# Weighted sums divided two banks at a time and added by GpSimd, in a two-layer graph attention kernel

## The chip, the cores and the metric

The kernel runs on one core of one Trainium2 chip. The metric is the device time of one execution in microseconds (us), the median of several runs. The kernel before was run three times: 2948.39, 2948.5 and 2950.46 us.

A core has five engines that work side by side, each through its own queue in order: TensorE (PE in the profile; its weight loads are PEld), VectorE (DVE), ScalarE (ACT), GpSimd (POOL) and SyncE (SP), which issues most of the transfers. The queues meet at semaphores: an instruction that waits holds up all that is queued behind it on its engine.

## The reference

The input x has 128 graphs of 64 nodes with 768 features, adj the 128 adjacency matrices of 64 x 64. All is fp32. Two layers follow each other, each with a residual and a layer norm.

```
layer 0:  p = softmax(h h^T / sqrt(768)) * adj;  attn = p / (sum(p) + 1e-10)
          ctx = upper(attn) (h Wl + bl) + diag(attn) (h Ws + bs) + lower(attn) (h Wr + br)
          x  = layernorm(x + relu(layernorm(ctx) * gamma + beta))
layer 1:  q, k, v = x Wq + bq, x Wk + bk, x Wv + bv       (12 heads of 64)
          s = q k^T / sqrt(64) + beta * adj;  s = -9e15 where adj is not > 0
          x  = layernorm(x + softmax(s) v)
```

## The kernel before

**Blocks.** The 8192 tokens are worked on in 16 blocks of 512 (four tiles t of 128 tokens, two graphs in a tile). The large products (self, left, right, values, queries and keys) are done with a seven-product scheme in place of eight: a block's transposed rows and each weight matrix are split in halves both ways, sums of the quarters are formed, and partial results in PSUM are shared. The sums of the rows (`combined`, L316 to L328) are made by GpSimd. For the left and right side the scheme is applied twice from the fourth block on: `both_sides` with `nested` (L419) has 49 sub-products (i, j), and `second_level` (L330) makes the second sums, q, on GpSimd, 13 blocks in all.

**The order of a block.** In the main loop (L1022 on) the stages of neighbouring blocks follow each other on TensorE: turn n of the loop has the two sides of block n+1 (left and right), its self product, the values of block n (with the context of block n+1 in between), and three projections of block n's queries and keys, one for each group of heads hg, four heads in each. A stage calls hooks at places that the loop lists (`at(left, 5, weighted, p, 1)`, with p = n-1): `scores`, `weighted` and `finish_by_act` of block p, transfers. Keys of the two-side stage run from 0 to 27 over its 49 sub-products; the places of `right` begin at 14.

In the two-side stage the matrices come in the order i = 7, 1, 2, 6, 5, 4, 3. The sub-products of one matrix are interleaved with those of the next: (i,6), (i,5), (i,7), then (next,1), (next,2), then (i,4), (i,3). Those with j = 1, 6, 7 are one matmul (two passes in the profile), the others two. Sub-products 1, 6, 7 and 4 of a matrix accumulate in one PSUM bank X, which is evicted after each; so (i,7) must wait until X is evicted after (i,6). Evictions are VectorE additions of 384 columns (L437).

**Queues of small work.** What belongs to other stages is put in three queues of entries, `first`, `urgent` and `lazy`, and `step` (L135), called after each sub-product, emits from them. Here "emits" means that the instruction gets its place in its engine's queue. The rules that matter: one step emits at most one plain entry (a piece of VectorE work), taken from the first queue that has one; entries of the kinds "act", "gap" and "tiny" may go along with it; after sub-products 5, 1 and 4 the step is light and emits no plain entry. "after" entries wait until `first` is empty. A gap entry does nothing but take a step.

**Scores (L814).** q k^T of four heads goes to two PSUM tiles; VectorE multiplies each with m8, the mask that also holds 1/8 (L836), and then, as entries of `urgent`, adds the second mask (L857), takes maxima (L858) and subtracts them (L859). ScalarE makes exponentials (L850), written so that two VectorE transposes (L854) end the turn.

**Weighted sums (L863).** The products of probabilities and values (with a column of ones for the denominators) go to four PSUM tiles of one bank, one for each pair of tiles h and head row r. Four entries of `first`, `added(h, r)`, follow, each a reciprocal of denominators and four operations that scale one head and add it to the rows:

```
nc.vector.reciprocal(rz, ps[:, :, :, HD])
...
nc.vector.scalar_tensor_tensor(res[:, r, c, hg, :], ps[:, t, k, 0:HD], rz[:, t, k : k + 1],
                               res[:, r, c, hg, :], ALU.mult, ALU.add)
```

**The last layer norm (`finish_by_act`, L894).** For the block before, ScalarE sums each of the four tiles ("after" entry, L934), VectorE makes the mean (L909, "tiny"), ScalarE sums squares (L937), VectorE the variance (L912, "tiny"), ScalarE a root, VectorE the factors (L918, L919), ScalarE norms the rows (L923), GpSimd issues the stores (L927). Two gaps stand between the sums and L909 and between the squares and L912. In the two-side stage it is queued at place 16, one place after the last `weighted` (place 15).

**Buffers.** `x1_p` holds the rows of two blocks, eight tiles. `wst` has 19 buffers for streamed weights. [...] `ps_st` four (X and Y, two each), `ps_mm` four one-bank buffers for scores, weighted sums, context, layer 0's products and transposes.

**Prologue.** Before the loop the weights are loaded, their quarters' differences are formed by VectorE (`prepare`, L192) and those for queries and keys are stored for streaming.

## Time and profile before

| | |
|---|---|
| median of three runs | 2948.5 us |
| profiled execution: its time, its span | 2945.44, 2943.7 us |
| TensorE clock granted, mean | 0.995 |
| TensorE matmuls busy | 98% of the span, 17578 instructions |
| VectorE busy | 1990.9 us, 68% |
| ScalarE busy | 1123.3 us, 38% |
| GpSimd busy | 729.8 us, 25% |
| L889, scale and add a head (VectorE) | 768 x 277 ns |
| L836, scores times mask (VectorE, 512 elements from PSUM) | 96 x 684 ns |
| L857, second mask (VectorE, 1024 elements) | 48 x 1221 ns |
| L451, addition on GpSimd, 384 elements | 52 x 1000 ns |
| period of a late block | 179.7 us |

The span is from the first instruction to the last, and 1.7 us of the execution lie around it. Busy times overlap. TensorE's matmuls are pipelined and their ends are modelled, so its 98% is read with care: what counts is the distance from one start to the next. A wait that the lists put down to an engine may belong to another semaphore that the instruction waits for as well; where the two could be mixed up, the timelines of the engines are laid side by side.

### The profile page before, as it was taken

The page shows a single profiled execution, that of the slowest core. Times are in us where ns is not written, and L with a number is a line of the kernel's source. Part 1 is how long each engine was busy: PE and PEld are TensorE (multiplying, and loading weights), DVE is VectorE, ACT ScalarE, POOL GpSimd, SP SyncE. Part 2 cuts the span into 40 slices and gives each one's busy share as a digit, 9 for nine tenths or more (in the row PEclk, how much of TensorE's full clock was granted, in tenths as well). Part 3 has the DMA queues.
Part 4 walks back from the last instruction along what each step waited for, and adds up shares of the span by engine and source line. Part 5 has one row for each costly group of instructions (what it writes and reads, how often), then busy time and mean ns, then how long its engine had stood idle before and what let it go on. Part 6 is the DMA issues. An engine that isn't in the chain of part 4 may idle for free.

```text
span 2943.7 us, 49954 instructions
## 1 busy us (share of the span) xinstructions
PE 2881.4 (98%) x17578; PEld 1935.1 (66%) x17578; DVE 1990.9 (68%) x4034; ACT 1123.3 (38%) x2114; POOL 729.8 (25%) x879
## 2 busy tenths in 40 slices
PE   8999999999999999999999999999999999999997
PEld 5557667575675856658576575766757567585685
DVE  5857777676676766767667576666767667676656
ACT  0004324344243542434434344443434424354254
POOL 3133122305123141321404124051230513313110
PEclk9999999999999999999999999999999999999998
DMA  9778786949669495775957759486694966849442
GB/s 329 222 247 266 230 247 181 266 135 284 160 193 248 138 292 152 207 237 157 277 149 231 216 168 271 138 254 188 183 262 136 287 158 196 247 136 289 139 127 90
DMA packets 440278, 613.18 MB, mean 208 GB/s; under 512 B 53584, under 2 KB 416720, under 8 KB 440032
## 3 DMA queue, kind: packets, MB, share of 16 engines
q1 hardware_dynamic: 362096, 493.57, 55.7%
q10 hardware_dynamic: 60848, 44.05, 8.1%
q0 software_dynamic: 17088, 72.37, 6.7%
q8 instruction: 143, 2.34, 0.3%
q14 instruction: 103, 0.84, 0.1%
HBM read 539.43 MB, written 77.27 MB: 209 GB/s over the span
## 4 chain that ended last, share of the span: by engine, by line
PE 90%; ACT 3%; DVE 3%; POOL 2%; DMA 2%; issue 1%; SPq 0%; DVEq 0%; ACTq 0%
PE ps_X L383 35%; PE ps_Y L383 26%; PE ps_Y L636 11%; PE ps_X L636 10%; PE ps_ctx L675 3%; ACT eT L850 2%; PE sc L832 2%; PE ps_y L879 2%; PE u L526 1%; POOL q L336 1%; ACT L850 1%; ACT uqk L801 1%; POOL q L335 0%; DVE o L889 0%; DMA bs<-in_L_gnn_b_self_dram 0%
## 5 line engine op out<-in xcount | busy, mean ns | idle before, releaser
L383 PE MATMUL ps_X<-xT,wqk 128*128 128x256 f32 x1728 | 395.9, 381 | 9.5 <-ACT uqk L801 9.5
L850 ACT ACTIVATE eT<-s 32x256 f32<-32x256 f32 x768 | 317.8, 414 | 184.7 <-DVE s L859 174.6
L383 PEld LDWEIGHTS ps_X<-xT,wqk 128*128 128x128 f32 x1728 | 325.8, 190 | 67.0 <-ACT uqk L801 16.2
L316 POOL TENSOR_TENSOR S<-hT 128x768 f32<-128x768 f32 x16 | 28.9, 1807 | 1132.9 <-PE ps_Y L383 1102.1
L383 PE MATMUL ps_Y<-S,wqk 128*128 128x256 f32 x1152 | 264.3, 379 | 0.0
L680 ACT ACTIVATE unused<-o 128x768 f32<-128x768 f32 x60 | 50.6, 844 | 499.6 <-DVE o L677 305.2
L383 PEld LDWEIGHTS ps_Y<-S,wqk 128*128 128x128 f32 x1152 | 218.9, 190 | 29.8
L437 DVE TENSOR_TENSOR lr<-ps_Y,u_deep 128x384 f32<-128x384 f32 x273 | 152.0, 557 | 107.5 <-PE ps_Y L636 81.4
L636 PE MATMUL ps_Y<-wlr,q 128*128 128x384 f32 x546 | 208.6, 491 | 0.0
L383 PE MATMUL ps_X<-wv,xT 128*128 128x384 f32 x576 | 195.0, 489 | 0.0
L801 ACT ACTIVATE uqk<-ps_X,bq 128x256 f32<-128x256 f32 x144 | 68.1, 473 | 325.1 <-PE ps_X L383 323.9
L383 PE MATMUL ps_X<-ws,hT 128*128 128x384 f32 x540 | 181.2, 490 | 2.8 <-DVE u L414 2.8
L809 DVE TENSOR_TENSOR q<-ps_Y,uqk 128x256 f32<-128x256 f32 x144 | 61.0, 423 | 178.0 <-ACT uqk L801 89.4
L889 DVE SCALAR_TENSOR_TENSOR o<-ps_y,rz,o 128x64 f32<-128x64 f32 x768 | 165.0, 277 | 6.8
L636 PE MATMUL ps_X<-wlr,q 128*128 128x384 f32 x364 | 151.0, 497 | 14.8 <-issue 6.2
L383 PEld LDWEIGHTS ps_X<-wv,xT 128*128 128x128 f32 x576 | 108.2, 190 | 80.8 <-issue 8.4
L383 PEld LDWEIGHTS ps_X<-ws,hT 128*128 128x128 f32 x540 | 103.2, 191 | 75.5 <-DVE u L414 3.4
L437 DVE TENSOR_TENSOR u_deep<-ps_X,lr 128x384 f32<-128x384 f32 x195 | 107.2, 550 | 67.4 <-PE ps_X L636 65.7
L636 PEld LDWEIGHTS ps_Y<-wlr,q 128*128 128x128 f32 x546 | 101.6, 190 | 67.2
L414 DVE TENSOR_TENSOR u<-ps_X,bv 128x384 f32<-128x384 f32 x96 | 53.4, 556 | 131.2 <-PE ps_X L383 131.2
L383 PE MATMUL ps_X<-S,wqk 128*128 128x256 f32 x576 | 138.2, 385 | 0.0
L383 PE MATMUL ps_Y<-xT,wqk 128*128 128x256 f32 x576 | 135.6, 385 | 0.0
(247 smaller groups left out, 5484.8 us busy)
## 6 DMA issues: line engine op xcount, KB each, us to landing
wlr<-lr_d SPq DMA_DIRECT2D x819, 192.0 KB, 3.4
wqk<-qk_d SPq DMA_DIRECT2D x672, 192.0 KB, 2.4
wv<-d_v SPq DMA_DIRECT2D x192, 192.0 KB, 2.9
ws<-d_s SPq DMA_DIRECT2D x180, 192.0 KB, 5.9
wv<-in_L_gnn_Wv_dram SPq DMA_DIRECT2D x144, 192.0 KB, 4.1
ws<-in_L_gnn_W_self_dram SPq DMA_DIRECT2D x135, 192.0 KB, 5.4
xa<-in_x_dram SPq DMA_DIRECT2D x64, 384.0 KB, 5.3
out_dram<-o POOLq DMA_DIRECT2D x62, 384.0 KB, 6.3
```

The source lines that it names most:

```text
L383: nc.tensor.matmul(ps, lhsT=a, rhs=b, start=(c == 0 and i in (1, 2, 5)), stop=(c == len(fs) - 1), skip_group_check=True)
L414: evicted[nm] = nc.vector.tensor_tensor(u, ps, bias[nm][:, b * HALF : (b + 1) * HALF], ALU.add)
L437: nc.vector.tensor_tensor(dst, view(ps), add, ALU.add)
L636: nc.tensor.matmul(ps, lhsT=a, rhs=b, start=(k == 0 and j in (1, 2, 5)), stop=(k == len(fs) - 1), skip_group_check=True)
L675: nc.tensor.matmul(ps[g * L : (g + 1) * L, 0:HALF], lhsT=blk["aT"][:, t, g * L : (g + 1) * L], rhs=blk["lr"][t][:, g, cols], start=True, s ...
L680: nc.scalar.activation(unused(), o[t], AF.Identity, accum_out=total[:, t : t + 1])
L801: nc.scalar.activation(u, ps, AF.Identity, bias=bias["qk"[j]][:, c : c + 1])
L809: nc.vector.tensor_tensor(dst, ps, part, ALU.add)
L832: nc.tensor.matmul(sc[r][g * L : (g + 1) * L, t, c, :], lhsT=q[rows, c, tok], rhs=k[rows, c, tok], start=True, stop=True)
L850: nc.scalar.activation(e[cols, :, rows], pairs[rows, :, cols], AF.Exp)
L879: nc.tensor.matmul(y[r, h][cols, t, c, :], lhsT=eT[rows, 2 * h + t, c, cols], rhs=v[rows, 2 * h + t, g, hg + c * HC, :], start=True, stop= ...
L889: nc.vector.scalar_tensor_tensor(res[:, r, c, hg, :], ps[:, t, k, 0:HD], rz[:, t, k : k + 1], res[:, r, c, hg, :], ALU.mult, ALU.add)
```

## The change

- `ps_mm` has two buffers of two banks in place of four of one bank; each user takes a pair (`two_banks`).
- `weighted`: one PSUM tile for each head row r, with both pairs of tiles. Two entries, `added(r)`: VectorE takes the reciprocals, multiplies all heads at once into a tile `shares` in SBUF, and GpSimd adds that to the rows.
- `scores`: the weights and the bias of the queries are scaled by 1/8 in the prologue (four ScalarE copies and a small VectorE operation). So VectorE adds one mask to the scores on the way out of PSUM; m8 and L857 fall away.
- Context: both halves of a tile in one pair of banks, one VectorE operation of 768 columns in place of two of 384.
- A block's rows are one tile of `x1_p` in place of four; `wst` has 17 buffers, not 19, which makes room for `shares`.

```diff
-    x1_p = ctx.enter_context(tc.tile_pool(name="x1_p", bufs=2 * T))
+    x1_p = ctx.enter_context(tc.tile_pool(name="x1_p", bufs=2))
...
-    wst = ctx.enter_context(tc.tile_pool(name="wst", bufs=19))
+    wst = ctx.enter_context(tc.tile_pool(name="wst", bufs=17))
...
-    ps_mm = ctx.enter_context(tc.tile_pool(name="ps_mm", bufs=4, space=PSUM))
+    ps_mm = ctx.enter_context(tc.tile_pool(name="ps_mm", bufs=2, space=PSUM))
...
+    nc.vector.tensor_scalar(bias["q"], bias["q"], 1.0 / math.sqrt(HD), None, ALU.mult)
...
+    def two_banks(name):
+
+        return ps_mm.tile([P, 2, 512], F32, tag="mm", name=name)
...
+        if nm == "q":
+
+            for q in b.values():
+                later(key, act(partial(nc.scalar.activation, q[1], q[1], AF.Copy, scale=1.0 / math.sqrt(HD))))
...
-        o = [x1_p.tile([P, D], F32, tag="x1", name=f"o_{n}_{t}") for t in range(T)]
+        blk["x_all"] = x1_p.tile([P, T, D], F32, tag="x1", name=f"o_{n}")
+        o = [blk["x_all"][:, t, :] for t in range(T)]
...
+            ps = two_banks("ps_ctx")[:, :, 0:HALF]
             for h in range(2):
                 cols = slice(h * HALF, (h + 1) * HALF)
-                ps = ps_mm.tile([P, 512], F32, tag="mm", name="ps_ctx")
...
-                nc.vector.scalar_tensor_tensor(o[t][:, cols], o[t][:, cols], dg[:, t : t + 1], ps[:, 0:HALF],
-                                               ALU.mult, ALU.add)
+            halves = o[t].rearrange("p (h c) -> p h c", h=2)
+            nc.vector.scalar_tensor_tensor(halves, halves, dg[:, t : t + 1], ps, ALU.mult, ALU.add)
...
         def one():
-            nc.vector.tensor_scalar(m8, at, 0.0, 1.0 / math.sqrt(HD), ALU.is_gt, ALU.mult)
             nc.vector.tensor_scalar(off, at, 0.0, MASKED, ALU.is_le, ALU.mult)
+            nc.vector.tensor_scalar(add, at, 0.0, abeta_c, ALU.max, ALU.mult)
...
-            nc.vector.tensor_tensor(s[:, :, :, r, :], sc[r], m8[:, :, None, :].to_broadcast([P, T, 2, L]), ALU.mult)
+            nc.vector.tensor_tensor(s[:, :, :, r, :], sc[:, r], add, ALU.add)
...
-              lambda: nc.vector.tensor_tensor(s4, s4, add[:, :, None, :].to_broadcast([P, T, 4, L]), ALU.add),
               lambda: nc.vector.tensor_reduce(mx, s8, AX.X, ALU.max),
...
-        y = {(r, h): ps_mm.tile([P, 2, 2, HD + 1], F32, tag="mm", name=f"ps_y{r}") for h in halves for r in range(2)}
+        y = [two_banks(f"ps_y{r}")[:, 0 : len(halves), 0 : 4 * (HD + 1)]
+             .rearrange("p h (t c d) -> p h t c d", t=2, c=2) for r in range(2)]
...
+        def added(r):
+            k = len(halves)
+            rz = st.tile([P, 2, 4], F32, tag="rz1", name="rz1")[:, 0:k, :]
+            shares = yt_p.tile([P, 2, 4, HD], F32, tag="shares", name="shares")[:, 0:k]
+            by_head = y[r].rearrange("p h t c d -> p h (t c) d")
+            nc.vector.reciprocal(rz, by_head[:, :, :, HD])
+            nc.vector.tensor_tensor(shares, by_head[:, :, :, 0:HD], rz[:, :, :, None].to_broadcast([P, k, 4, HD]),
+                                    ALU.mult)
+            res = blk["x_all"][:, 2 * halves[0] : 2 * halves[0] + 2 * k, :]
+            res = res.rearrange("p t (c k r d) -> p t r c k d", c=2, k=HC, r=2)[:, :, r, :, hg, :]
+            nc.gpsimd.tensor_tensor(res, res, shares.rearrange("p h (t c) d -> p (h t) c d", c=2), ALU.add)
+
+        later(("y", n, hg), *[partial(added, r) for r in range(2)], queue=first)
...
+    yt_p = ctx.enter_context(tc.tile_pool(name="yt", bufs=2))
```

More of the change, by code (lines that the diff above doesn't have):

```diff
@@ L280, in transposed @@
     def transposed(src, xT, t):
+        both = two_banks("ps_x").rearrange("p b (c i) -> p b c i", c=4)
         for c0 in range(0, KC, 3):
-            ps = ps_mm.tile([P, 4, P], F32, tag="mm", name="ps_x")
+            ps = both[:, c0 // 3]
             for c in range(3):
@@ L519, in attention0 @@
         freed()
-        u = ps_mm.tile([P, T, L], F32, tag="mm", name=f"u_{n}")
+        u = two_banks(f"u_{n}")[:, 0, 0 : T * L].rearrange("p (t l) -> p t l", t=T)
         for t in range(T):
@@ L574, in sides @@
         freed()
-        aps = ps_mm.tile([P, T, P], F32, tag="mm", name="ps_a")
+        aps = two_banks("ps_a")[:, 0, :].rearrange("p (t m) -> p t m", t=T)
         for t in range(T):
@@ L670, in part @@
             freed()
+            ps = two_banks("ps_ctx")[:, :, 0:HALF]
             for h in range(2):
                 cols = slice(h * HALF, (h + 1) * HALF)
-                ps = ps_mm.tile([P, 512], F32, tag="mm", name="ps_ctx")
                 for g in range(2):
-                    nc.tensor.matmul(ps[g * L : (g + 1) * L, 0:HALF], lhsT=blk["aT"][:, t, g * L : (g + 1) * L],
+                    nc.tensor.matmul(ps[g * L : (g + 1) * L, h, :], lhsT=blk["aT"][:, t, g * L : (g + 1) * L],
                                      rhs=blk["lr"][t][:, g, cols], start=True, stop=True)
-                nc.vector.scalar_tensor_tensor(o[t][:, cols], o[t][:, cols], dg[:, t : t + 1], ps[:, 0:HALF],
-                                               ALU.mult, ALU.add)
+            halves = o[t].rearrange("p (h c) -> p h c", h=2)
+            nc.vector.scalar_tensor_tensor(halves, halves, dg[:, t : t + 1], ps, ALU.mult, ALU.add)
             if by_act:
@@ L742, in mask @@
         at = blk["at"]
-        m8 = l0.tile([P, T, L], F32, tag="m8", name=f"m8_{n}")
-        add = l0.tile([P, T, L], F32, tag="add", name=f"add_{n}")
+        blk["add"] = add = l0.tile([P, T, L], F32, tag="add", name=f"add_{n}")
         off = l0.tile([P, T, L], F32, tag="a", name="off")
-        blk["m8"], blk["add"] = m8, add
         def one():
-            nc.vector.tensor_scalar(m8, at, 0.0, 1.0 / math.sqrt(HD), ALU.is_gt, ALU.mult)
             nc.vector.tensor_scalar(off, at, 0.0, MASKED, ALU.is_le, ALU.mult)
+            nc.vector.tensor_scalar(add, at, 0.0, abeta_c, ALU.max, ALU.mult)
         def two():
-            nc.vector.tensor_scalar(add, at, 0.0, abeta_c, ALU.max, ALU.mult)
             nc.vector.tensor_add(add, add, off)
@@ L824, in scores @@
         s = l1s_p.tile([P, T * 4 * L], F32, tag="s", name="s").rearrange("p (t c r m) -> p t c r m", t=T, c=2, r=2)
-        sc = [ps_mm.tile([P, T, 2, L], F32, tag="mm", name=f"sc{r}") for r in range(2)]
+        sc = two_banks("sc").rearrange("p r (t c m) -> p r t c m", t=T, c=2)
         for t in range(T):
@@ L831, in scores @@
                         tok = slice(t * P + g * L, t * P + (g + 1) * L)
-                        nc.tensor.matmul(sc[r][g * L : (g + 1) * L, t, c, :], lhsT=q[rows, c, tok],
+                        nc.tensor.matmul(sc[g * L : (g + 1) * L, r, t, c, :], lhsT=q[rows, c, tok],
                                          rhs=k[rows, c, tok], start=True, stop=True)
-        m8, add = blk["m8"], blk["add"]
+        add = blk["add"][:, :, None, :].to_broadcast([P, T, 2, L])
         for r in range(2):
-            nc.vector.tensor_tensor(s[:, :, :, r, :], sc[r], m8[:, :, None, :].to_broadcast([P, T, 2, L]), ALU.mult)
-        s4 = s.rearrange("p t c r m -> p t (c r) m")
+            nc.vector.tensor_tensor(s[:, :, :, r, :], sc[:, r], add, ALU.add)
         s8 = s.rearrange("p t c r m -> p (t c r) m")
@@ L861, in scores, with weighted @@
               *([partial(turn, 0), partial(turn, 1)] if pool is None else [lambda: (turn(0), turn(1))]), queue=urgent)
-    def weighted(n, hg, halves=range(2), heads=range(2)):
+    def weighted(n, hg, halves=(0, 1)):
         blk = blocks[n]
@@ L869, in weighted @@
         freed()
-        xt, eT = blk["x"], blk["eT", hg]
-        y = {(r, h): ps_mm.tile([P, 2, 2, HD + 1], F32, tag="mm", name=f"ps_y{r}") for h in halves for r in range(2)}
-        for h in halves:
+        eT = blk["eT", hg]
+        y = [two_banks(f"ps_y{r}")[:, 0 : len(halves), 0 : 4 * (HD + 1)]
+             .rearrange("p h (t c d) -> p h t c d", t=2, c=2) for r in range(2)]
+        for k, h in enumerate(halves):
             for t in range(2):
-                for c in heads:
+                for c in range(2):
                     for r in range(2):
@@ L878, in weighted @@
                             cols = slice(g * L, (g + 1) * L)
-                            nc.tensor.matmul(y[r, h][cols, t, c, :], lhsT=eT[rows, 2 * h + t, c, cols],
+                            nc.tensor.matmul(y[r][cols, k, t, c, :], lhsT=eT[rows, 2 * h + t, c, cols],
                                              rhs=v[rows, 2 * h + t, g, hg + c * HC, :], start=True, stop=True)
-        def added(h, r):
-            ps = y[r, h][:, :, heads[0] : heads[-1] + 1, :]
-            rz = st.tile([P, 2, 2], F32, tag="rz1", name="rz1")[:, :, 0 : len(heads)]
-            nc.vector.reciprocal(rz, ps[:, :, :, HD])
-            for t in range(2):
-                res = xt[2 * h + t].rearrange("p (c k r d) -> p r c k d", c=2, k=HC, r=2)
-                for k, c in enumerate(heads):
-                    nc.vector.scalar_tensor_tensor(res[:, r, c, hg, :], ps[:, t, k, 0:HD], rz[:, t, k : k + 1],
-                                                   res[:, r, c, hg, :], ALU.mult, ALU.add)
-        later(("y", n, hg), *[partial(added, h, r) for h in halves for r in range(2)], queue=first)
+        def added(r):
[10 more added lines that the diff above has]
+        later(("y", n, hg), *[partial(added, r) for r in range(2)], queue=first)
     def finish_by_act(n, tiles=range(T), queue=urgent):
```

## The prediction

> **What bounds the kernel now.** I read the page's busy times first, then the list of waits for TensorE alone, then the timeline of one late block, engine by engine.

> ```profile
> span 2943.7 us, 49954 instructions
> PE 2881.4 (98%) x17578; PEld 1935.1 (66%) x17578; DVE 1990.9 (68%) x4034; ACT 1123.3 (38%) x2114; POOL 729.8 (25%) x879
> ```

> ```profile
> PE ps_X L383 <- ACT uqk L801: 9.5, 16, 0.6
> PE ps_X L383 <- DVE u L414: 8.2, 4, 2.8
> ```

> TensorE sets the time, its matmul count does not change, and VectorE is not the bound on average. So 200 us less VectorE work buys only the small waits of TensorE. In a late block (period 179.7 us) I find them by spacing. A matmul of 384 columns is issued each 0.32 us; what is longer is a wait. Timeline at sub-products (5,6), (5,5), (5,7) of the stage of the two sides, TensorE, then VectorE (start, length in us):

> ```profile
> 1784.88 0.81 PE L636 MATMUL ps_X<-wlr,q 128*128 128x384 f32 x2
> 1785.53 0.81 PE L636 MATMUL ps_Y<-wlr,q 128*128 128x384 f32 x2
> 1786.17 0.81 PE L636 MATMUL ps_Y<-wlr,S 128*128 128x384 f32 x2
> 1787.19 0.88 PE L636 MATMUL ps_X<-wlr,q 128*128 128x384 f32 x2 [0.21 <-issue]
> ...
> 1785.76 0.86 DVE L889 SCALAR_TENSOR_TENSOR o<-ps_y,rz,o 128x64 f32<-128x64 f32 x4
> 1786.54 0.55 DVE L437 TENSOR_TENSOR u_deep<-ps_X,lr 128x384 f32<-128x384 f32 x1
> ```

> The last matmul should come at 1786.82 and comes at 1787.19: 0.37 late, because it accumulates on a bank whose eviction (1786.54) stood behind the additions of the weighted sum. The same reading, at each eviction that follows a sub-product (i,3), gives four such waits a block: behind additions 0.37 twice (before 1762.99 and 1787.19), behind the L859 subtraction 0.62 (before 1770.78), behind a transpose 0.40 (before 1778.4). One wait of 0.76 in the third projection is for ScalarE, busy with exponentials. The rest of a block's waits the change does not touch.

> The chain that ends the previous block's layer norm shares these queues:

> ```profile
> 1788.49 0.84 ACT L934 ACTIVATE unused<-o 128x768 f32<-128x768 f32 x1 [11.42 <-DVE o L889]
> 1792.14 0.19 ACT L934 ACTIVATION_READ_ACCUMULATOR unused<-o 128x1 f32 x1
> 1793.09 0.94 ACT L937 ACTIVATE unused<-o,f 128x768 f32<-128x768 f32 x1 [0.76 <-DVE f L909]
> 1797.12 0.18 ACT L937 ACTIVATION_READ_ACCUMULATOR unused<-o,f 128x1 f32 x1
> ...
> 1791.33 0.56 DVE L437 TENSOR_TENSOR lr<-ps_X,lr 128x384 f32<-128x384 f32 x1
> 1792.36 0.69 DVE L909 TENSOR_SCALAR f<-f 128x4 f32<-128x4 f32 x1 [0.47 <-ACT unused L934]
> 1795.87 0.56 DVE L437 TENSOR_TENSOR lr<-ps_Y,u_deep 128x384 f32<-128x384 f32 x1
> 1797.33 0.21 DVE L912 TENSOR_SCALAR f<-f 128x4 f32<-128x4 f32 x1 [0.91 <-ACT unused L937]
> ```

> The small VectorE steps L909 and L912 are queued just late enough: each waits under 1 us for ScalarE's four sums (3.84 us) and four squares (4.2 us).

> [...] the trace gives 1000 ns for 384 elements (L451) and 1807 for 768 (L316), 2.1 ns per element[...] in the two stretches that hold 2.8 us waits (columns: stretch, length, busy times, granted clock):

> ```profile
> 130.00:142.00 12.00, 9.23 (x24) 5.01 (x23) 10.93 (x21) 0.00 (x0) 0.00 (x0) 0.86 1.09 297
> 162.00:176.00 14.00, 11.21 (x26) 6.01 (x26) 9.60 (x12) 0.00 (x0) 13.34 (x18) 0.76 1.05 386
> 36.00:40.00 4.00, 1.99 (x6) 0.88 (x6) 3.93 (x9) 0.00 (x0) 2.27 (x5) 1.00 1.01 370
> ```

> The last one, with 2.0 us idle, keeps its clock.

> **The change part by part.**
> *Weighted sums.* Per block and head group VectorE loses 4 reciprocals (172 ns) and 16 operations (277 ns) and gets 2 reciprocals and 2 products of 512 elements (684, from L836): 5.12 to 1.71 us. GpSimd gets 2 additions of 512; from L451 and L316 1.27 us each, 122 us in all. An entry of the queue `first` falls from 0.98 us of VectorE (rz to the next operation in the timeline) to 0.81 (0.21, and 0.60, half of the 1.29 us pair of L836 less overlap), and there are two entries, not four.
> *Mask.* L857 (1221 ns, 48) and L749 go; one entry of the chain of scores goes with it.
> *Context.* Two operations of 614 become one of about 1016 (L704 has that size): 13 us of VectorE in all, hidden under TensorE's value products.
> These three free 200 us of VectorE; only the named waits are on the path. Played through the queues' rules, the steps now emit L857 after (7,7), L858 (1,2), additions (7,3) (1,6) (1,7) (2,2), L859 (1,3), exponentials (2,6) (2,5), transposes (2,3) (6,6), additions (5,2) (6,3) (5,6) (5,7), and the timeline has them there. Changed: L858 (7,7), L859 (1,2), additions (7,3) (1,6), exponentials (7,3) (1,6), transposes (1,3) (2,6), additions (5,2) (6,3). What stands before the four evictions, after (7,3), (1,3), (2,3) and (6,3), becomes additions, transpose, nothing, additions. So 0.37+0.62+0.40+0.37 becomes 0.20+0.14+0+0.20 (each shorter by what is shorter in front): 1.2 us gained. In the third projection the exponentials start one step (1.3 us) earlier, but three groups of 1.7 stand before the eviction in place of two: 0.76 becomes about 0.3. Gain per block 1.67; bounds 0.8 and 2.1.

> *What is late next.* Two entries fewer pull the layer-norm chain forward by three sub-products: the sums are queued after (6,3), not (5,7); L909 after (5,7), not (5,4); L912 after (5,3), not (4,7). ScalarE cannot follow. Count from (5,6) at 0. VectorE's second product ends at 1.55, GpSimd's addition, behind L452 (0.33) and the first one, at 2.95; ScalarE is free of its own DMA issues at 3.2 to 3.6 (1788.4 in the trace). Sums end 3.87 later: L909 starts at 6.85 to 7.5 (call it T). It stands in VectorE's queue since 4.05, ahead of the evictions of (4,1), (4,2), (5,4), (5,3). L909 0.2 to 0.6, squares 4.24, so L912 ends at about T+4.7 to T+5.1; only then comes the eviction of (4,6) with 0.65, which (4,7) needs. (4,7) starts at 12.2 to 13.2, against 9.23 undisturbed (sub-products of one matmul, 0.645 us, or two from 2.13 on). Loss 3.0 to 4.0 us in a block; I take 3.5. The gaps are about 0.8 before (4,6) and 2.6 before (4,7).
> Net 3.5 - 1.67 = 1.83 us, in the 13 blocks with this stage: +24. The first two blocks and the last have the projection's gain alone: -2.

> *GpSimd's queue.* The two late additions (2.5 us) stand before the second-level sums of matrices 4 and 3, where GpSimd idles some 1 us between 1781.9 and 1799.1; the last sums come 1.5 to 1.9 us late against a slack of about 1.4: 0 to 0.6 a block. The 3.5 us above cover it; without that cover it is 8 us in all. The early two have idle time (3.69 us before 1768.47).
> *Pairs of banks, two buffers.* Each pair is evicted several us before its slot comes round (scores at 1752.9, next use 1758.2): 0; in the tail, where weighted sums follow each other, -1 to +1.
> *One tile for a block's rows.* The first write (1811.66) now waits for all four stores, issued up to 1803.5 with a median of 6.3 to landing: 0, and VectorE has two steps of slack behind it.
> *17 weight buffers.* Some 0.9 us per tile (63 in 57 us), so 1.8 us less lead; landing takes 3.4 (median), and the waits list shows TensorE waiting for none of these loads: 0, bound +1 a block.
> *Query weights scaled.* Four ScalarE copies of 1152 elements in the prologue, ScalarE idle there but VectorE's differences wait for them: 0 to 3, I take 1. *Tail*: the last addition through GpSimd, +0.8.
> *Clock.* A gap of 2.6 lies between 2.0 (no drop) and 2.8 (drop). A drop costs 1.7 (0.14 x 12) to 3.4 us (0.24 x 14). I expect it in few blocks: +2.

> Sum: 24-2+1+1+2 = +26 on the profiled 2945.4 (span and 1.7 around it), which lies 3.1 below the median of 2948.5: forecast 2974.5, 0.9% slower. A measurement here tells about 0.2% from no change.

> **Rivals.**
> (1) Faster: the layer-norm chain does not block, only the gains show: -1.67 x 13 - 2 = -24, 2925. For it: all the waits of VectorE above are real. Against: ScalarE's 3.87 us of sums cannot fit in the 2.8 us between their new place and L909's. It decides if L909 stays queued behind (5,3); the loss is nought where T is below 3.4 to 3.9.
> (2) GpSimd becomes the bound of the stage: 31 us busy of 57 there, 36 after; with the gains kept and 0.6 lost a block, 2933[...].
> (3) The clock drops in every block: 13 x 2.5 more, 3005. For it: the gap is close to 2.8.
> (4) The shallower weight ring starves TensorE at the stage's end, where transfers crowd: 1 us a block more, 2987.

> **How the numbers follow.** Forecast with few drops 0.60 (its own range 2962 to 2990: losses 3.0 to 4.0, gains 0.8 to 2.1); (3) 0.11; (4) or another added loss 0.07; (1) 0.12; (2) 0.10, split evenly between faster and no change. Slower 0.78, same 0.05, faster 0.17. The range 2930 to 3004 leaves out most of (1) and the worst of (3).

> **What would show it.** Right: in the timeline L909 waits 2 to 3 us on L934 and L912 about as long on L937, with a TensorE gap of some 2.6 us before each (4,7); L885 in pairs; VectorE near 1790 us busy, GpSimd near 850. Wrong: L909 behind (5,3), TensorE's period at 178, or waits for `wlr`, `q` or ScalarE's `uqk` in its list.

## The result and the profile after

The changed kernel takes 3020.5 us, the median of four runs (3018.1 to 3022.4), beside 2949.0 of the kernel before on the same chip: a ratio of 1.0241, with a 95% interval from 1.0224 to 1.0259. The forecast was 2974.5 with a range up to 3004. The sign was right and the size was not: +72 us where +26 was forecast.

The page of the changed kernel, the span and the busy times:

```profile
span 3017.7 us, 49120 instructions
PE 2907.4 (96%) x17578; PEld 1941.9 (64%) x17578; DVE 1830.7 (61%) x3151; ACT 1129.4 (37%) x2120; POOL 828.0 (27%) x981
```

VectorE has lost 160 us of work, GpSimd has gained 98, and TensorE, with the same number of matmuls, has a span 74.0 us longer. Its list of waits (total, times, longest) shows what the time went to:

```profile
PE ps_X L647 <- DVE u_deep L447: 36.0, 26, 2.6
PE ps_X L647 <- POOL lr L461: 11.6, 13, 0.9
PE ps_X L393 <- DVE u L424: 10.5, 5, 3.5
PE ps_X L393 <- ACT uqk L810: 9.1, 31, 1.5
...
PE ps_y L887 <- DVE shares L896: 5.8, 3, 4.5
PE ps_y L887 <- DVE rz L895: 4.5, 4, 2.4
```

The first two stand in the stage of the two sides (L647 is L636 of the kernel before, L447 is L437) and come in each of its 13 blocks, the first twice, once for 2.6 us and once for 0.2. The last two stand in the tail. I measured the stages from the first product of one to the first product of the next in TensorE's record:

| part of the run | before | after | difference |
|---|---|---|---|
| up to the first nested two-side stage | 490.5 | 496.6 | +6.1 |
| the 13 two-side stages, sum | 735.1 | 788.7 | +53.6 |
| a late two-side stage | 56.5 | 60.9 | +4.4 |
| projections of a block | 62.5 | 62.4 | -0.1 |
| projections of the last block | 124.0 | 128.4 | +4.4 |
| tail, from the last values on | 54.7 | 65.4 | +10.7 |
| period of a late block | 179.7 | 184.05 | +4.3 |

In the timeline of one late block, VectorE and then TensorE, the forecast steps are all there (L919 is the mean, L922 the variance; the last number in brackets is the idle time before the instruction):

```profile
1637.61 0.56 DVE L447 TENSOR_TENSOR lr<-ps_Y,u_deep 128x384 f32<-128x384 f32 x1
1640.78 1.04 DVE L919 TENSOR_SCALAR f<-f 128x4 f32<-128x4 f32 x1 [2.62 <-ACT unused L944]
1641.74 0.54 DVE L447 TENSOR_TENSOR u_deep<-ps_X,lr 128x384 f32<-128x384 f32 x1
...
1646.10 0.50 DVE L922 TENSOR_SCALAR f<-f 128x4 f32<-128x4 f32 x1 [2.23 <-ACT unused L947]
1646.51 0.54 DVE L447 TENSOR_TENSOR u_deep<-ps_X,lr 128x384 f32<-128x384 f32 x1
...
1642.38 0.88 PE L647 MATMUL ps_X<-wlr,q 128*128 128x384 f32 x2 [0.89 <-POOL lr L461]
1643.10 0.81 PE L647 MATMUL ps_Y<-wlr,q 128*128 128x384 f32 x2
1643.75 0.81 PE L647 MATMUL ps_Y<-wlr,hT 128*128 128x384 f32 x2
1647.11 1.34 PE L647 MATMUL ps_X<-wlr,q 128*128 128x384 f32 x2 [2.56 <-DVE u_deep L447]
1648.25 1.49 PE L647 MATMUL ps_X<-wlr,S 128*128 128x384 f32 x2
```

VectorE holds L919 for 2.62 us while ScalarE sums, and the eviction at 1641.74 stands behind it; TensorE starts (4,6) 1.05 us late. The list names GpSimd's L461 for that wait, but that ended at 1641.80 and the eviction at 1642.28, just ahead of the matmul at 1642.38. L922 then holds the next eviction, and (4,7) comes 2.72 us late.

What the forecast did not count in every block is in the spacing of the two last rows: two matmuls of 384 columns each, 1.14 us apart where 0.64 is usual. Here are the 3.41 us that hold most of the wait, and the 3.41 us after them (columns: stretch, length, busy times of PE, PEld, DVE, ACT and POOL, granted clock, DMA share, GB/s; the last section says why this length):

```profile
1644.06:1647.47 3.41, 0.85 (x3) 0.30 (x2) 0.96 (x2) 3.35 (x6) 3.33 (x4) 1.00 0.90 288
1647.47:1650.88 3.41, 3.41 (x7) 1.76 (x6) 2.08 (x5) 0.72 (x2) 3.01 (x6) 0.50 0.88 323
```

After the wait the granted clock is 0.50, and TensorE has 7 matmuls in the stretch. Waits of the same length in two of the 13 blocks let the clock stand; after one of them it has 12:

```profile
1278.81:1282.22 3.41, 1.50 (x5) 0.98 (x6) 1.45 (x3) 2.34 (x4) 3.25 (x5) 1.00 0.99 332
1282.22:1285.64 3.42, 3.42 (x12) 1.98 (x11) 2.46 (x7) 2.44 (x3) 2.71 (x6) 1.00 1.00 362
```

Those two stages take 59.2 us, the others 60.9 (one 61.3). The fall costs 1.7 us.

### The profile page after: what moved, and what is told of

Its sections match the earlier page's. It is cut to its first block, busy times and chain, and to the rows that moved or that the text cites. A ratio compares the mean times of both kernels' runs of the same rounds, so it can differ in the third digit from the quotient of the medians.

```text
span 3017.7 us, 49120 instructions
## 1 busy us (share of the span) xinstructions
PE 2907.4 (96%) x17578; PEld 1941.9 (64%) x17578; DVE 1830.7 (61%) x3151; ACT 1129.4 (37%) x2120; POOL 828.0 (27%) x981
## 3 DMA queue, kind: packets, MB, share of 16 engines
q1 hardware_dynamic: 362096, 493.57, 54.7%
## 4 chain that ended last, share of the span: by engine, by line
PE 77%; ACT 11%; DVE 5%; DMA 5%; issue 1%; POOL 0%; SPq 0%; ACTq 0%; DVEq 0%
PE ps_X L393 30%; PE ps_Y L393 23%; PE ps_Y L647 9%; PE ps_X L647 8%; ACT eT L858 5%; PE ps_ctx L686 3%; ACT unused L947 2%; PE sc L841 2%; DMA wlr<-lr_d 2%; ACT unused L944 2%; PE u L536 1%; ACT uqk L810 1%; PE ps_y L887 1%; DMA sq<-x1d 1%; ACT L858 1%
## 5 line engine op out<-in xcount | busy, mean ns | idle before, releaser
L900 POOL TENSOR_TENSOR o<-o,shares 128x512 f32<-128x512 f32 (+1 forms) x102 | 126.4, 1248 | 1388.6 <-DVE shares L896 1309.7
L858 ACT ACTIVATE eT<-s 32x256 f32<-32x256 f32 x768 | 317.8, 414 | 48.3 <-DVE s L866 37.6
L691 ACT ACTIVATE unused<-o 128x768 f32<-128x768 f32 x60 | 50.6, 843 | 507.0 <-DVE o L689 264.9
L447 DVE TENSOR_TENSOR lr<-ps_Y,u_deep 128x384 f32<-128x384 f32 x273 | 152.1, 557 | 140.1 <-PE ps_Y L647 116.9
L647 PE MATMUL ps_Y<-wlr,q 128*128 128x384 f32 x546 | 208.6, 491 | 0.0
L647 PE MATMUL ps_X<-wlr,q 128*128 128x384 f32 x364 | 153.9, 505 | 48.7 <-DVE u_deep L447 33.2
L944 ACT ACTIVATE unused<-o 128x768 f32<-128x768 f32 x62 | 52.3, 843 | 288.2 <-POOL o L900 164.6
L447 DVE TENSOR_TENSOR u_deep<-ps_X,lr 128x384 f32<-128x384 f32 x195 | 107.3, 550 | 82.6 <-PE ps_X L647 80.3
L647 PEld LDWEIGHTS ps_Y<-wlr,q 128*128 128x128 f32 x546 | 100.5, 190 | 68.3 <-DVE lr L447 4.5
L647 PEld LDWEIGHTS ps_X<-wlr,q 128*128 128x128 f32 x364 | 64.0, 190 | 115.8 <-DVE u_deep L447 41.2
```

The costliest lines, as they stand in the source:

```text
L447: nc.vector.tensor_tensor(dst, view(ps), add, ALU.add)
L647: nc.tensor.matmul(ps, lhsT=a, rhs=b, start=(k == 0 and j in (1, 2, 5)), stop=(k == len(fs) - 1), skip_group_check=True)
L691: nc.scalar.activation(unused(), o[t], AF.Identity, accum_out=total[:, t : t + 1])
L858: nc.scalar.activation(e[cols, :, rows], pairs[rows, :, cols], AF.Exp)
L900: nc.gpsimd.tensor_tensor(res, res, shares.rearrange("p h (t c) d -> p (h t) c d", c=2), ALU.add)
L944: later(key, (partial(sums, lambda t, o: nc.scalar.activation(o, xt[t], AF.Identity, accum_out=total[:, t : t + 1])), "after"), GAP, GAP, ...
```

## The experiments

**1. The chain put back to its place.** Three more gap entries between the sums and the mean.

```diff
-              GAP, GAP, tiny(mean),
+              *[GAP] * 5, tiny(mean),
```

> The changed kernel with three more gap entries between the sums and the mean in finish_by_act, which puts the mean (L919) and the variance (L922) back to the places of the kernel before, after (5,4) and (4,7). Theory (the early chain makes the two waits and the half clock behind the second): in the changed kernel they cost 1.05 + 2.72 + 1.77 = 5.5 us in a late block, so 13 blocks give back 68 to 72 us: 2946 to 2956, and a late block's period is 178.5 to 179 us. Rival A (GpSimd, with the additions now on it, is late with the second-level sums, and bounds the stage as soon as VectorE's waits are gone): at most 2 us a block come back, 2994 or more, with waits for GpSimd in TensorE's list. Rival B (17 weight buffers): no change, 3015 to 3025.

Measured: 2965.2 us, ratio 1.0057 (1.0042 to 1.0072). The period of a late block is 178.99, the two-side stage takes 55.85, so the 13 stages cost 726 us where the changed kernel has 789 and the kernel before 735. Of the two waits nothing is left. The mechanism holds, and rivals A and B fall: with the chain late enough, the additions on GpSimd and the ring of 17 leave a block shorter than before. The timeline shows also what A was right about, TensorE, then GpSimd:

```profile
1803.67 0.91 PE L647 MATMUL ps_X<-wlr,q 128*128 128x384 f32 x2 [0.32 <-POOL q L346]
...
1788.97 2.67 POOL L900 TENSOR_TENSOR o<-o,shares 128x512 f32<-128x512 f32 x2
...
1802.63 0.46 POOL L345 TENSOR_TENSOR q<-S 128x128 f32<-128x128 f32 x1
1803.17 0.45 POOL L346 TENSOR_TENSOR q<-q,S 128x128 f32<-128x128 f32 x1
```

The two additions of 2.67 us make the second-level sums of a later matrix late, and TensorE waits 0.49 us for L346, once a block. In the changed kernel the longer waits covered it.

The total missed its expectation by 9 us, for two reasons outside the 13 stages. In turn 1 of the loop the self product of block 2 (the expectation of run 7 calls it block 1) takes 33.3 us, not 27.1, and VectorE shows why:

```profile
387.21 1.02 DVE L601 TENSOR_TENSOR o<-ps_Y,u 128x384 f32<-128x384 f32 x2 [8.22 <-DMA out_dram<-o]
```

The rows of a block are one tile now, and the first write to them waits for all four stores of block 0. The gap entries delay those stores, and block 0's chain has no nested stage to run in. The other is the tail, 68.7 for 65.4, where the same entries stand in the last chains.

**2. The variance alone, one place later.**

```diff
-              GAP, GAP, tiny(variance), act(root), ...
+              *[GAP] * 3, tiny(variance), act(root), ...
```

> The changed kernel with one more gap entry between the squares and the variance, nothing else. The variance is then queued after (4,6), behind that sub-product's eviction. It waits for ScalarE as before, but what stands behind it is needed three sub-products later. Theory with the clock as a cost of its own: the wait before (4,7) goes, and the half clock that follows it too: 13 x (2.72 + 1.77) = 58, so 2962 (2955 to 2970); the wait of 1.05 before (4,6) stays. If the clock's fall has another cause than that wait: 13 x 2.72 = 35, 2985. If the wait only moves to the next eviction: 3010 or more.

Measured: 2962.8 us, ratio 1.0051 (1.0036 to 1.0066). The two-side stage takes 56.6 us, 4.3 less than 60.9: the wait of 2.72 and the 1.7 of half clock went together (the granted clock of the profiled run is 0.993, that of the changed kernel's 0.988). VectorE, then TensorE:

```profile
1798.60 0.55 DVE L447 TENSOR_TENSOR u_deep<-ps_X,lr 128x384 f32<-128x384 f32 x1
1800.91 0.51 DVE L922 TENSOR_SCALAR f<-f 128x4 f32<-128x4 f32 x1 [1.76 <-ACT unused L947]
...
1798.56 0.81 PE L647 MATMUL ps_Y<-wlr,hT 128*128 128x384 f32 x2
1799.20 0.91 PE L647 MATMUL ps_X<-wlr,q 128*128 128x384 f32 x2
```

VectorE still waits 1.76 us at L922. But the eviction that (4,7) needs stands ahead of it, and (4,7) starts at 1799.20, on time. The wait of 1.05 before (4,6), which the edit does not touch, is still there.

**3. The mean one place later,** and with it all that follows.

```diff
-              GAP, GAP, tiny(mean),
+              *[GAP] * 3, tiny(mean),
```

> The changed kernel with one more gap entry between the sums and the mean, which moves the mean behind the eviction of (4,1) and the variance behind that of (4,6). Theory (a wait costs what the next needed eviction behind it loses, not what the waiting instruction waits): both instructions still wait 2 to 3 us on VectorE, but both waits of TensorE go, so it is within 8 us of the kernel with three more entries, 2946 to 2964. If instead the length of VectorE's wait counts, about a third of the gain of three entries comes: 2995 to 3000.

Measured: 2973.4 us, ratio 1.0080 (1.0063 to 1.0097), between the two expectations and nearer the first. The stage takes 56.9 us for most blocks. VectorE waits as long as ever, 2.15 us at L919 and 2.42 at L922 in the block read, and the waits before (4,6) and (4,7) are gone; but a new one of 1.01 stands three sub-products on, before (4,4), whose bank waits for an eviction behind L922, and one of 0.35 before (4,5). So an entry moved by one place takes most of the loss, but a piece of it moves to the next eviction. The right side of block 2 takes 33.9 us for 31.1 besides. Against 2, a later mean makes the squares, and so the variance, later. In the 13 stages that is some 3 of the 11 us between the two runs; that right side makes 6 of them (28.0 in 2), and the last of the 13 stages takes 59.1, with one wait of 1.8 us for weights.

**4. The chain pulled forward in the kernel before,** which leaves out two of the last weighted sum's four entries, so that the chain comes earlier by two.

```diff
-        later(("y", n, hg), *[partial(added, h, r) for h in halves for r in range(2)], queue=first)
+        later(("y", n, hg), *[partial(added, h, r)
+              for h in (halves if hg != 2 or not DEEP - 2 <= n < NBLK - 2 else (0,)) for r in range(2)], queue=first)
```

> The kernel before with two of the four entries of the last weighted sum (hg 2) left out in the 13 blocks with the two-side stage nested: half of that head group's sums are not added to the rows. VectorE has 2 us less work in a block; nothing else of the change is made. The chain's sums, mean and variance are then queued after (6,3), (5,7) and (5,3), as in the changed kernel. Theory: the waits come with the places alone. The sums begin up to 1 us earlier than in the changed kernel, since no addition goes through GpSimd, so a block loses 2 to 5.5 us: 2975 to 3020. Rivals A and B: 2940 to 2950, no loss without the additions on GpSimd and the shallower ring.

Measured: 2996.9 us, ratio 1.0166 (1.0151 to 1.0182): with less work than the kernel before it takes 48 us more. The stages take 58.3 to 61.5 us, 783 in all. TensorE in a late block:

```profile
1820.29 0.81 PE L636 MATMUL ps_Y<-wlr,hT 128*128 128x384 f32 x2
1823.65 1.59 PE L636 MATMUL ps_X<-wlr,q 128*128 128x384 f32 x2 [2.56 <-DVE u_deep L437]
1825.03 1.49 PE L636 MATMUL ps_X<-wlr,S 128*128 128x384 f32 x2
```

The same wait of 2.72 before (4,7), and the spacing of half clock behind it (the last two rows start 1.38 us apart where 0.64 is usual; the granted clock of the run is 0.990, 0.995 in the kernel before), without a pair of banks, an addition on GpSimd or a shallower ring. So the number of entries ahead of the chain is enough to make the loss of the blocks.

**5. Pairs of banks alone, in the kernel before.** Each user of `ps_mm` takes a pair; the context keeps its operation for each half.

```diff
+            both = two_banks("ps_ctx")
             for h in range(2):
-                ps = ps_mm.tile([P, 512], F32, tag="mm", name="ps_ctx")
+                ps = both[:, h]
                 ... two products, then one scalar_tensor_tensor on ps
```

> The kernel before with ps_mm as two buffers of two banks, each user taking a pair, and nothing else of the change (four entries of a weighted sum, two masks, additions by VectorE). The prediction's value: 0, tail -1 to +1, so 2948 to 2950. Against it, from the trace of the changed kernel: transposes that wait for two evictions of a pair (prologue +2.4, last block +4.4) and weighted sums of one half in the tail, which follow each other and take a pair for each head row (+3 to +6): 2957 to 2963, with the blocks' period at 179.7 as before.

Measured: 3019.3 us, ratio 1.0240 (1.0226 to 1.0254). That is as slow as the whole change, and for another reason, as the stages show: the two sides take 56.5 as before, the values 37.5 where both kernels have 33.6. The first entry of TensorE's list of waits, and the place in the timeline:

```profile
PE ps_ctx L681 <- DVE o L683: 46.5, 61, 1.8
```

```profile
1871.89 0.87 PE L681 MATMUL ps_ctx<-lr,aT 128*64 128x384 f32 x4
1873.50 0.87 PE L681 MATMUL ps_ctx<-lr,aT 128*64 128x384 f32 x4 [0.74 <-DVE o L683]
```

The products of the second half wait until VectorE has read the first half in the other bank of the pair. The change avoids this by its one operation for a tile. So this run did not measure the pairs as the change uses them, and the agreement of its total with the changed kernel's is chance.

**6. 17 weight buffers alone, in the kernel before.**

```diff
-    wst = ctx.enter_context(tc.tile_pool(name="wst", bufs=19))
+    wst = ctx.enter_context(tc.tile_pool(name="wst", bufs=17))
```

> The kernel before with 17 buffers for streamed weights in place of 19, nothing else. Theory: no wait for weights, 2946 to 2952 and a period of 179.7. Rival (the shallower ring starves TensorE at the stage's end): 1 us a block, 2962.

Measured: 2946.2 us, ratio 0.9993 (0.9984 to 1.0001). A late period is 179.8. The 13 stages take 737.2 us for 735.1, with two waits for weights of 0.6 us at most: the ring costs next to nothing and is not the cause.

**7. The tail's additions on VectorE,** with the chain put back in the 13 blocks only (and one gap entry more before the variance of block 0).

```diff
+        deep = queue is urgent and len(tiles) == T and n + 2 >= DEEP
-              GAP, GAP, tiny(mean),
+              *[GAP] * (5 if deep else 2), tiny(mean),
-              GAP, GAP, tiny(variance), ...
+              *[GAP] * (3 if n == 0 else 2), tiny(variance), ...
-            nc.gpsimd.tensor_tensor(res, res, shares ...
+            (nc.gpsimd if k == 2 else nc.vector).tensor_tensor(res, res, shares ...
```

What it is aimed at is in the changed kernel's tail, TensorE, GpSimd, VectorE:

```profile
2995.58 0.48 PE L887 MATMUL ps_y<-v,eT 64*64 64x65 f32 x4 [0.71 <-DVE rz L895]
3000.60 1.13 PE L887 MATMUL ps_y<-v,eT 64*64 64x65 f32 x28 [4.54 <-DVE shares L896]
...
2997.08 2.16 POOL L937 DMA_DIRECT2D out_dram<-o  x4 [4.13 <-ACT o L933]
2999.26 2.09 POOL L900 TENSOR_TENSOR o<-o,shares 128x256 f32<-128x256 f32 x3
...
3000.03 0.42 DVE L896 TENSOR_TENSOR shares<-ps_y,rz 128x256 f32<-128x256 f32 x1 [4.51 <-POOL o L900]
```

Four stores that wait for ScalarE stand on GpSimd's queue ahead of the additions; `shares` has two buffers, so VectorE's next product waits, and TensorE's next weighted sum for that.

> The changed kernel with three more gap entries before the mean in the 13 blocks with the nested stage, one before the variance of block 0, and the additions of the weighted sums of one half (tail only) made by VectorE in place of GpSimd. Blocks: period 179.0 as in the first experiment, without its loss of 6 in block 1: some 2955 to 2958 with the tail as it was. Theory for the tail (an addition on GpSimd stands behind four stores that wait for ScalarE, and the next product waits for `shares`): the wait of 4.5 us goes, and 0.5 to 1 for each detour: tail from 65.4 to 59 to 61, the whole 2950 to 2954. Rival (the pairs of banks are what the tail waits for): tail 64 to 65, 2954 to 2958.

Measured: 2952.3 us, ratio 1.0015 (1.0008 to 1.0022). The blocks do what was expected (period 179.0; block 2's self product back at 27.1), and the 4.5 us are gone. But the tail takes 63.1, not 59 to 61: with that wait away, the pairs hold it. In this run's tail, TensorE:

```profile
2929.97 0.48 PE L887 MATMUL ps_y<-v,eT 64*64 64x65 f32 x4 [0.64 <-DVE shares L896]
2930.98 1.13 PE L887 MATMUL ps_y<-v,eT 64*64 64x65 f32 x28 [0.53 <-DVE shares L896]
2932.76 0.48 PE L887 MATMUL ps_y<-v,eT 64*64 64x65 f32 x4 [0.64 <-DVE shares L896]
```

A weighted sum of one half takes both pairs, one for each head row, so each waits twice for the one before it to be read.

**8. All mended.** As 7, and a weighted sum of one half takes one pair for both head rows; transposes go to the four banks of `ps_st`.

```diff
+        if len(halves) == 2:
             y = [two_banks(f"ps_y{r}") ... for r in range(2)]
+        else:
+            one = two_banks("ps_y")
+            y = [one[:, r : r + 1, 0 : 4 * (HD + 1)] ... for r in range(2)]
...
-        both = two_banks("ps_x") ...
-            ps = both[:, c0 // 3]
+            ps = ps_st.tile([P, 512], F32, tag="XY"[c0 // 3], name="ps_x") ...
```

> As the run before, and besides: a weighted sum of one half takes one pair of banks for both head rows in place of two, and transposes go to the four banks of ps_st, one tile of three in each, as many as in the kernel before. Theory: last block's projections back from 128.4 to 124.0, prologue's values from 36.0 to 33.6, tail to 54 to 57: with a period of 179.0 in place of 179.7 and some 3 us more in the prologue, 2934 to 2944, 0.2 to 0.5% below the kernel before. If pairs cost nothing there: as the run before, 2950 to 2954.

Measured: 2936.9 us, beside 2948.1: ratio 0.9958 (0.9945 to 0.9972), faster than both kernels. The last projections take 125.1, the prologue's values 33.6, the tail 57.0, all down from 128.4, 36.0 and 63.1, so the pairs were the cause there. Of the last projections 1.1 us, and of the tail 2.3, are left above the kernel before. The scaled query weights and the 17 buffers are still in it, and the first nested stage starts at 488.4, earlier than the kernel before's 490.5: neither costs anything here that can be seen.

**9. Pairs alone, with the context as the change has it.** As 5, with one operation for both halves.

> The kernel before with pairs of banks, as in the run of pairs alone, but with one VectorE operation of 768 columns for both halves of a context tile, as the change has it. Theory (in the run of pairs alone the second half's products waited for the first half's reading, some 4 us in each of 15 stages of values, a wait that the one operation removes): values back at 33.6 us, two sides at 56.5 and a period of 179.7 as before. What is left is the pairs' own cost at the ends: last projections 127.4 for 124.0, tail 66 for 54.7, prologue 3 to 6: 2960 to 2970. If the wait of the values comes from the pairs as such: 3010 or more.

Measured: 2959.7 us, ratio 1.0037 (1.0023 to 1.0051). The values are back at 33.6, the two sides stand at 56.5, the period at 179.75. The pairs cost only where work that uses them follows itself: the tail takes 66.4 for 54.7 and the last projections 127.4 for 124.0, since four transposes there wait 0.76 each for the two copies of a pair. TensorE in this run's tail:

```profile
2939.96 0.48 PE L888 MATMUL ps_y<-v,eT 64*64 64x65 f32 x4 [1.08 <-DVE rz L894]
2940.94 1.13 PE L888 MATMUL ps_y<-v,eT 64*64 64x65 f32 x28 [0.50 <-DVE o L898]
```

No addition goes through GpSimd here, and the tail is no shorter than the changed kernel's 65.4. By 9 the pairs alone make a tail as long, though the wait of 4.5 us for GpSimd was real: what each costs depends on which is taken away first.

## Why the prediction was wrong

**The mechanism and its place: right.** L919 and L922 wait 2.6 and 2.2 us on ScalarE, and (4,6) and (4,7) come 1.05 and 2.72 us late, where about 0.8 and 2.6 were forecast. Loss without the clock: 3.77 us, inside 3.0 to 4.0. Run 4 shows that the earlier places alone make it, run 1 that the places of before take it away.

**The clock: the term that failed most.** The step "a gap of 2.6 lies between 2.0 (no drop) and 2.8 (drop) ... I expect it in few blocks: +2" was a reading between two points by the length of the wait, and it fell on the wrong side: the clock fell to 0.50 in 11 of 13 blocks, at 1.7 us each, 19 us. The price was right (1.7 to 3.4 was stated); the count was not. It was rival (3), given 11 in 100. In the changed kernel's trace the length alone did not decide: all 13 waits hold some 2.56 us of idle time, and what differed was how much of it lay in one stretch of 3.41 us, 2.07 or more in the 11, 1.90 and 1.80 in the other two (last section).

**The gain of the blocks: half of it went.** The evictions gained what was forecast: waits of 1.76 us became 0.60, 1.16 for 1.2. But the projections gained 0.1 us for 0.45: in the third one the wait of 0.76 for ScalarE fell to 0.38, near the 0.3 forecast, and a new one of 0.41 for ScalarE stands in the second. And with the chain at its old place a wait of 0.49 for GpSimd's L346 appears. The prediction had priced that one, at 0 to 0.6 a block, and named its cover, so in the changed kernel it adds nothing to the loss. Run 1's period is 0.75 us below the kernel before, where 1.67 was forecast for the gain alone.

For the blocks: 3.77 of waits, less 1.16, and 1.7 x 11/13 = 1.44 of clock is 4.05 a stage, 52.7 for 13 stages; measured 53.6. The forecast's terms for these stages were 3.5 less 1.22, 30 for 13, and 2 for the clock.

**Pairs of banks: the second step that failed, at the ends.** "In the tail ... -1 to +1" and "the last addition through GpSimd, +0.8" stand against +10.7, and nothing was put down for the last block's projections, which took 4.4 more. The step looked at the distance to a slot's next use in the middle of the run, where it holds (run 9: period unchanged), and not at the places where sums of one half, or transposes, follow each other. A sum of one half takes half of each of two pairs, and so has as many slots as one sum. In the tail the clock is at half for 28.8 us (17.5 in the kernel before); what that costs there is within these figures and was not separated.

**The prologue: +6.1 where -2 for the first two blocks and the last, and +1 for the query weights, stood.** Two parts are seen. The right side of block 2 takes 31.1 us for 27.1: there too the variance holds an eviction while ScalarE is late, by a wait of 2.19 and the half clock after it (granted clock 0.50 from 364.04 to 367.46). In run 2, where the variance comes one place later, it takes 28.0. The prediction looked for the chain in the nested stages only. The values of block 0 take 36.0 for 33.6, which runs 8 (33.6 without pairs for the transposes) and 9 (36.0 with the pairs alone) put to the pairs. The rest, shifts of 1 to 4 us both ways, I have not followed; the right side of block 0, which the edits of runs 1 to 3 do not touch, differs by up to 4.5 us between them and the changed kernel (36.1 to 40.6).

**The sum.** Of the 46 us between forecast and result, by these figures, about 17 are clock in the 13 stages, 14 the tail and the last projections, 5 the stages beyond that, 5 the projections' missing gain and 5 the rest of the prologue. None of them closes the gap alone.

**The rest.** VectorE is busy for 1830.7 us where near 1790 was forecast, GpSimd for 828 where 850 was; neither is on the path, and I have not followed the difference. The ring of 17 cost next to nothing (run 6), as forecast. One tile for a block's rows cost nothing in the changed kernel, but that is no property of the edit: when run 1 made the stores later, it cost 6 us in block 2. Rival (1), faster, is what the same edits give once the chain is put back and the pairs are mended (run 8): 11 us, not the 24 of the gains as forecast.

## What to carry to other kernels

Before an entry is taken out of a shared queue, play the queue forward to the next entry that waits for another engine: the entries ahead of it were its delay. What such a wait costs is not its length but how soon the work queued behind it is needed; one place can be worth 4 us a block, as in run 2. A change of buffers is to be checked where the work that uses them comes back to back, at the ends of the run, and not only at its steady distance.
